# State-space scan kernel: finer preparation of a segment, a second buffer for each product with C, du * B a step ahead, side loads two slots ahead

## Chip, cores and metric

The kernel runs on one core of one Trainium2 chip. The metric is the device time of one execution in microseconds. Every profile line comes from one profiled execution; TensorE is called PE, VectorE DVE, ScalarE ACT, GpSimd POOL, and SP is the engine whose queue issues the DMAs.

## What is computed

The reference is a network of four layers over four images of 64 x 64 positions with 96 channels. Layers 0 and 1 are selective state-space blocks: a projection, a depthwise 3 x 3 convolution with SiLU, four scans over the positions (rows and columns, each forwards and backwards), a layer norm, a gate and an output projection. Layer 1 works on a Fourier transform of the image. Layers 2 and 3 are linear attention and a feed-forward net on the tokens. Nearly all time goes into the scans, which compute for each channel, with 16 states n:

```
delta = softplus(dts + bias)
h[n]  = h[n] * exp(delta * A[n]) + delta * u * B[n]
y     = sum over n of h[n] * C[n]
```

All is float32 but parts of layers 2 and 3.

## The kernel before

**Phases.** The function `scans` runs six phases: two for layer 0 (each holds a pair of images, 64 channels of each on the 128 partitions at a time) and four for layer 1 (one image each). Each phase has four scan directions, each cut into segments: eight of 512 positions in layer 0, and 512, 512, 384, 384 and 320 in layer 1. That makes 144 segments. Ahead of the first phase and behind the last, the function `alone` runs work that no scan goes beside.

**Steps.** A segment has 12 steps: four quarters `q` of four states each, by three chunks `c` of channels. In each step, DVE runs four scans (L537): two write `hx`, the states 4q and 4q + 1, two write `hy`, the other two. POOL multiplies `hx` by C into `hcx` (L672), DVE multiplies `hy` by C into `hcy` (L692), and PE adds both, transposed, to the accumulator in PSUM (`accumulate`, L559). The two halves get du * B in different ways. For `hy`, POOL multiplies `du` by a broadcast B straight into the `hy` tile, which the scan then overwrites (`front_b`, L532). For `hx`, ACT scales a transposed copy of `du` by B into `bx` (`make_bx`, L489) for all three chunks of a quarter, and PE transposes it back into PSUM one step ahead (`transposed`, L509). ACT makes the exponentials (L514). POOL keeps the last state of a segment for the next one (`keep_state`, L550).

**Preparation.** While a segment is scanned, the generator `prepare` makes the next one ready: it loads `u` (L418), projects it (PE, L424), copies the result out and stores it (ACT L427, SP L428), makes `delta` (PE L433, ACT L435), takes its softplus, with one table load before and one behind it (L437, L438), transposes B (L443, L447), multiplies `du` (DVE, L451) and transposes that (PE L457, ACT L460). Each `yield` ends a piece.

**Side work.** Projections, the norm and gate, the Fourier transforms and the token layers of other images run as a second generator beside the scans, through `Env.step`. `E.defer` puts an eviction off to the next piece.

**What sets the order.** The four computing engines take their instructions in the order in which this code records them (`manual_schedule`); DMAs on SP are placed by a scheduler as early as their inputs and buffers allow. A step has three slots. In each one, `slot` runs a piece of side work when the phase's rate (`RATES`, a third of it a slot) has gathered to 1. `prepare_more` runs a piece of preparation, before the second and third slots. A generator that has yielded `LATE` goes on only in the third slot, and one that has yielded `BURST` only in `burst`, between the two scans of `hx`. The pieces of `make_bx` are taken in two handfuls a step (`take`); what is left in the last step of a quarter is drained at once, just ahead of the transposes that read it. A pool's tile has one buffer unless `bufs` says more: so with `hx`, `hy`, `hcx` and `hcy`, while `ax` and `delta` have two and `bx` four.

Of the kernel before, what the change touches and what calls it, by code (L numbers as in the profile page):

```python
# [6 lines left out]
F32 = mybir.dt.float32  # L7
# [15 lines left out]
SM = 512  # L23
LATE, BURST = "late", "burst"

RATES = [0.67, 1.37, 2.4, 1.64, 1.64, 1.64]
EXP_LN = "natural_log_exp_and_others"


# [66 lines left out]
class Block:  # L96
# [57 lines left out]
    def project(self, E, g, xf, out):  # L154
# [9 lines left out]
        with E.pool(f"{cfg.pre}pj{g}") as sp:  # L164
            for c in range(C):
# [4 lines left out]
                for p0, p1 in cfg.parts:  # L170
# [8 lines left out]
                    def visits(blocks, half, done):  # L179

                        nxt = load(*blocks[0], half)
                        for b, (r, n) in enumerate(blocks):
                            x, nxt = nxt, load(*blocks[b + 1], half) if b + 1 < len(blocks) else None
                            pi = E.psum(f"pi{half}_{nm}_{r}")
                            self.in_proj(pi, wi, half, x, n * 64)
                            E.defer(lambda r=r, n=n, pi=pi: done(r, n, pi))
                            yield
# [76 lines left out]
    def gated(self, E, g, io, out_proj):  # L264
# [5 lines left out]
        with E.pool(f"{cfg.pre}nm{g}") as sp:  # L270
# [18 lines left out]

            todo = iter(tiles)  # L290
            nxt = load(*next(todo))
            yield
            for b, (r, nr) in enumerate(cfg.rows):
                n = nr * 64
# [91 lines left out]
def scans(tc, ctx, phases, ident):  # L386
# [21 lines left out]
    def prepare(z):  # L408


        blk, cfg, k, S, nm = z.blk, z.cfg, z.k, z.S, z.nm
        rows = cfg.NI * cfg.M

        def room():
            return ps.tile([P, 512], F32, name=f"pp_{nm}", tag="pp")

        z.u = u = sp.tile([P, C, SM], F32, name=f"us_{nm}", tag="us")
        nc.sync.dma_start(out=u[:, :, :S], in_=z.ph.io["u"][k % 2][:, :, z.a : z.a + S])  # L418
        z.xd = blk.dram_tile("xd", (rows, SM), nm, bufs=4)
        yield  # L420
        yield
        px = room()
        for c in range(C):
            nc.tensor.matmul(px[:rows, :S], blk.xpw[:, c, k, :], u[:, c, :S], start=(c == 0), stop=(c == C - 1))  # L424
        yield
        xs = sp.tile([P, SM], F32, name=f"xs_{nm}", tag="xs", bufs=2)
        nc.scalar.copy(xs[:rows, :S], px[:rows, :S])  # L427
        nc.sync.dma_start(out=z.xd[:, :S], in_=xs[:rows, :S])  # L428
        yield
        z.delta = sp.tile([P, C, SM], F32, name=f"delta_{nm}", tag="delta", bufs=2)  # L430
        for c in range(C):
            pd = room()
            nc.tensor.matmul(pd[:, :S], blk.dtw[:, k, c * P : (c + 1) * P], xs[:rows, :S], start=True, stop=True)  # L433
            yield
            nc.scalar.activation(z.delta[:, c, :S], pd[:, :S], AF.Identity, bias=blk.dtb[:, c, k : k + 1])  # L435
        yield BURST
        nc.scalar.activation(z.delta[:, :, :S], z.delta[:, :, :S], AF.Softplus)  # L437
        nc.scalar.preload_act_table_set(EXP_LN)  # L438
        yield
        pb = room()  # L440
        pbv = pb[:, : NBK * rows].rearrange("p (b m) -> p b m", b=NBK)
        for i, (t, n) in enumerate(z.blocks):
            nc.tensor.transpose(pbv[:n, i, :], xs[:rows, t : t + n], ident[:rows, :rows])  # L443
        z.bt = sp.tile([P, NBK, rows], F32, name=f"bt_{nm}", tag=f"bt{cfg.pre}", bufs=2)
        yield
        for lo, hi, n in z.runs:
            nc.scalar.copy(z.bt[:n, lo:hi, :], pbv[:n, lo:hi, :])  # L447
        yield
        yield
        z.du = sp.tile([P, C, SM], F32, name=f"du_{nm}", tag="du", bufs=2)  # L450
        nc.vector.tensor_tensor(z.du[:, :, :S], z.delta[:, :, :S], u[:, :, :S], ALU.mult)  # L451
        yield
        z.dut = sp.tile([P, NBK, C, P], F32, name=f"dut_{nm}", tag="dut", bufs=2)
        for c in range(C):
            pt = room().rearrange("p (b d) -> p b d", b=NBK)
            for i, (t, n) in enumerate(z.blocks):
                nc.tensor.transpose(pt[:n, i, :], z.du[:, c, t : t + n], ident)  # L457
            yield
            for lo, hi, n in z.runs:
                nc.scalar.copy(z.dut[:n, lo:hi, c], pt[:n, lo:hi, :])  # L460
# [37 lines left out]
    def drain(gen):  # L498
        for _ in gen:
            pass  # L500
# [96 lines left out]
    with tc.manual_schedule(engines=IN_ORDER):  # L597
        drain(prepare(segs[0]))
        drain(make_bx(segs[0], 0))
        fetch(segs[0], 0)  # L600
        st = steps[0]
        st.px, st.ay = [transposed(st, j) for j in range(2)], {}
        front_x(st)
        front_b(st)
        front_y(st, 0)
        closing = None
        bgen, pgen, pwants, at, due = none, none, None, 0, 0.0

        def prepare_more(kind):

            nonlocal pwants
            if pwants not in (None, kind):
                return False
            pwants = next(pgen, LATE)
            return True

        def slot(kind):

            nonlocal due
            due = min(due + st.z.ph.rate / 3, 3.0)  # L620
            if due >= 1.0:
                due -= E.step(kind)

        def burst():

            if pwants is BURST:
                return prepare_more(BURST)
            if E.wants is BURST:
                E.step(BURST)
                return True  # L630
            return False

        for i, st in enumerate(steps):
            z, q, c, S = st.z, st.q, st.c, st.z.S
            nxt = steps[i + 1] if i + 1 < len(steps) else None
            if q == 0 and c == 0:
                after = segs[at + 1] if at + 1 < len(segs) else None
                if at == 0 or z.ph is not segs[at - 1].ph:
                    if closing:
                        close_chunk(closing)  # L640
                        closing = None
                    z.ph.io["y"] = [z.blk.dram_tile(f"y{j}", (2, z.cfg.L, C * P), z.ph.g) for j in range(2)]
                    E.start(z.ph.side(E))
                open_segment(z, segs[at - 1] if at else None)
                if after and after.ph is not z.ph:
                    E.finish()
                pgen, pwants = prepare(after) if after else none, None
                at += 1
            if c == 0:
                if q + 1 < NQ:  # L650
                    bgen = make_bx(z, q + 1)
                    fetch(z, q + 1)
                elif after:
                    drain(pgen)
                    bgen = make_bx(after, 0)
                    fetch(after, 0)
            per = -(-2 * z.cfg.NI * NBK // C)
            hx = sp.tile([P, 2, SM], F32, name=f"hx_{st.nm}", tag="hx")
            scan(st, hx, 0, st.ax[:, 0], st.px[0], 4 * q)
            front_y(st, 1)  # L660
            if nxt:
                nxt.ay = {}
                front_x(nxt)
            long = burst()
            scan(st, hx, 1, st.ax[:, 1], st.px[1], 4 * q + 1)
            slot(None)
            if nxt:
                if c == C - 1:
                    drain(bgen)
                nxt.px = [transposed(nxt, 0)]  # L670
            hcx = sp.tile([P, 2, SM], F32, name=f"hcx_{st.nm}", tag="hcx")
            nc.gpsimd.tensor_tensor(hcx[:, :, :S], hx[:, :, :S], z.c[q][0][:, :, :S], ALU.mult)  # L672
            keep_state(st, hx, 4 * q)
            first = 0 if long else per - per // 2
            take(bgen, first)
            scan(st, st.hy, 0, st.ay[0], st.hy[:, 0], 4 * q + 2)
            if nxt:
                nxt.px.append(transposed(nxt, 1))
            prepare_more(None)
            slot(None)  # L680
            scan(st, st.hy, 1, st.ay[1], st.hy[:, 1], 4 * q + 3)
            keep_state(st, st.hy, 4 * q + 2)
            if nxt:
                front_y(nxt, 0)
            take(bgen, per - first)
            if closing:
                close_chunk(closing)
            accumulate(st, hcx, 4 * q)
            prepare_more(None)
            slot(LATE)  # L690
            hcy = sp.tile([P, 2, SM], F32, name=f"hcy_{st.nm}", tag="hcy")
            nc.vector.tensor_tensor(hcy[:, :, :S], st.hy[:, :, :S], z.c[q][1][:, :, :S], ALU.mult)  # L692
            if nxt:
                front_b(nxt)
            accumulate(st, hcy, 4 * q + 2)
            closing = st if q == NQ - 1 else None
        close_chunk(closing)
        E.finish()
# [548 lines left out]
```

## Time and profile before

| What | Value |
|---|---|
| Median of 3 runs | 13097.33 us |
| Lowest and highest run | 13086.38 and 13113.72 us |
| Span of the profiled execution | 13109.2 us |
| Mean clock granted to TensorE | 0.841 of full speed |
| First scan starts, last step ends (about) | 528 us, 12551 us |
| POOL L532, du * B into hy | 1728 instructions, 3707.7 us |
| POOL L672, hx * C into hcx | 1637 under this name, 3556.9 us |
| DVE L692, hy * C into hcy | 1636 under this name, 1935.3 us |
| ACT L489, bx | 6272 instructions, 2760.0 us |

The page of the profile gives for each engine the time in which it was busy. For each group of instructions it gives their number, their total and mean duration, and the time in which the engine stood idle just ahead of them, together with the instruction whose end released it. A name such as `hcx_l<-hx_l,bc_l` reads output from inputs, with buffer numbers left out. Since a name that the tracer cuts in another place makes a group of its own, some groups are split (`b_l`, `ab_l`, or `cy_l` for a part of `hcy`). A wait of an engine that others don't wait for costs nothing; so a wait is weighed by what it does to the engine that is full.

### The profile page before, as it was taken

The numbers are of one execution on the slowest core, as the hardware profiler recorded it, in microseconds if no ns is written. First come the engines' busy times: TensorE is split into PE (matmuls) and PEld (weight loads), VectorE is DVE, ScalarE is ACT, GpSimd is POOL, SyncE is SP. The second block draws the span as 40 slices with busy tenths as digits, with TensorE's granted clock in tenths as the row PEclk, the third lists the DMA queues.
The fourth block names the chain that finished last, engine by engine and source line by source line (L and its number), as shares of the span: only waits on it lengthen the run. The fifth ranks groups of instructions, "written<-read, shape, count | busy, mean of one in ns | idle before, by whom it ended". The sixth has DMA issues, their size and how long they took to land. (4 is left out here: it accounts for less than half of the span.)

```text
span 13109.2 us, 165038 instructions
## 1 busy us (share of the span) xinstructions
PE 10013.8 (76%) x54680; PEld 7250.2 (55%) x54680; DVE 10549.6 (80%) x10170; ACT 9044.4 (69%) x17333; POOL 9139.5 (70%) x6620
## 2 busy tenths in 40 slices
PE   5677777777777888777888878877788777887766
PEld 1355555555665656556666555555556555555544
DVE  1398999999999888898776588898988989889833
ACT  1478888887777777886566677677676776767723
POOL 0398888888888887887556577676776767766620
PEclk8788888888888998888888889787887778887775
DMA  4444444444554545444444334322343224332231
GB/s 117 109 127 118 121 121 120 118 115 119 134 139 122 122 127 124 133 118 144 132 115 111 117 127 124 103 82 81 122 119 103 80 80 133 113 101 80 77 96 26
DMA packets 1264705, 1464.41 MB, mean 112 GB/s; under 512 B 494243, under 2 KB 1027055, under 8 KB 1255143
## 3 DMA queue, kind: packets, MB, share of 16 engines
q1 hardware_dynamic: 1263847, 1453.85, 39.6%
q8 instruction: 431, 7.06, 0.2%
q14 instruction: 427, 3.50, 0.1%
HBM read 1217.05 MB, written 236.50 MB: 111 GB/s over the span
## 5 line engine op out<-in xcount | busy, mean ns | idle before, releaser
L532 POOL TENSOR_TENSOR hy_l<-du_l,bc_l 128x1024 f32<-128x1024 f32 (+2 forms) x1728 | 3707.7, 2146 | 1710.9 <-DVE hcy_l L692 1261.0
L672 POOL TENSOR_TENSOR hcx_l<-hx_l,bc_l 128x1024 f32<-128x1024 f32 (+2 forms) x1637 | 3556.9, 2173 | 819.4 <-PE acc_l L559 654.6
L489 ACT ACTIVATE bx_l<-dut_l,bt_l 128x192 f32<-128x192 f32 (+2 forms) x6272 | 2760.0, 497 | 0.2
L692 DVE TENSOR_TENSOR hcy_l<-hy_l,bc_l 128x1024 f32<-128x1024 f32 (+2 forms) x1636 | 1935.3, 1183 | 392.4 <-PE acc_l L559 278.3
L559 PE MATMUL acc_l<-ident,hcy_l 128*128 128x128 f32 (+1 forms) x12120 | 1902.1, 306 | 363.0 <-DVE hcy_l L692 359.9
L514 ACT ACTIVATE ax_l<-delta_l,l_alog 128x512 f32<-128x512 f32 (+2 forms) x3456 | 2139.0, 667 | 0.0
L514 ACT ACTIVATE b_l<-delta_l,l_alog 128x512 f32<-128x512 f32 (+2 forms) x1961 | 1230.4, 628 | 1246.7 <-DVE hx_l L537 809.6
L537 DVE TENSOR_TENSOR_SCAN hy_l<-b_l,state_l,hy_l 128x512 f32<-128x512 f32 (+2 forms) x1697 | 1861.4, 1131 | 284.5 <-POOL hy_l L532 136.4
L559 PE MATMUL acc_l<-ident,hcx_l 128*128 128x128 f32 (+1 forms) x12126 | 1973.8, 314 | 86.5 <-POOL hcx_l L672 81.0
L559 PEld LDWEIGHTS acc_l<-ident,hcy_l 128*128 128x128 f32 (+1 forms) x12120 | 1606.3, 159 | 687.1 <-DVE hcy_l L692 488.2
L537 DVE TENSOR_TENSOR_SCAN hx_l<-ax_l,state_l,b_l 128x512 f32<-128x512 f32 (+2 forms) x1697 | 1839.7, 1125 | 164.1 <-PE b_l L509 132.2
L559 PEld LDWEIGHTS acc_l<-ident,hcx_l 128*128 128x128 f32 (+1 forms) x12126 | 1637.3, 161 | 520.1 <-issue 243.6
L509 PE MATMUL b_l<-ident,bx_l 128*128 128x128 f32 x6872 | 1262.3, 307 | 682.8 <-DVE hy_l L537 312.0
L514 ACT ACTIVATE ab_l<-delta_l,l_alog 128x512 f32<-128x512 f32 x1314 | 906.7, 690 | 937.7 <-DVE hx_l L537 637.4
L550 POOL COPY state_l<-hy_l 128x2 f32<-128x2 f32 x1392 | 1242.0, 892 | 373.2 <-DVE hy_l L537 283.4
L509 PEld LDWEIGHTS b_l<-ident,bx_l 128*128 128x128 f32 x6872 | 859.9, 154 | 1147.4 <-DVE hy_l L537 375.3
L509 PE MATMUL ab_l<-ident,bx_l 128*128 128x128 f32 x5260 | 944.6, 310 | 672.7 <-DVE hy_l L537 255.3
L537 DVE TENSOR_TENSOR_SCAN hy_l<-ab_l,state_l,hy_l 128x512 f32<-128x512 f32 x978 | 1206.2, 1270 | 126.2 <-POOL hy_l L532 75.8
L537 DVE TENSOR_TENSOR_SCAN hx_l<-ax_l,state_l,ab_l 128x512 f32<-128x512 f32 x979 | 1197.8, 1264 | 79.7 <-PE ab_l L509 69.3
L509 PEld LDWEIGHTS ab_l<-ident,bx_l 128*128 128x128 f32 x5260 | 656.1, 155 | 977.4 <-DVE hx_l L537 325.9
L225 PE MATMUL pc_l<-pad_l,l_dg 128*128 128x512 f32 (+2 forms) x1944 | 852.4, 582 | 60.0 <-ACT uh_l L214 43.7
L146 PE MATMUL pi_l<-xi_l,l_wi 96*128 96x384 f32 (+6 forms) x912 | 393.8, 717 | 286.7 <-DMA xi_l<-xn 131.0
(190 smaller groups left out, 12475.2 us busy)
## 6 DMA issues: line engine op xcount, KB each, us to landing
bc_l<-l_xd_l SPq DMA_DIRECT2D x1536, 256.0 KB
bc_l<-l_xd_l SPq DMA_DIRECT2D x384, 512.0 KB
bc_l<-l_xd_l SPq DMA_DIRECT2D x384, 384.0 KB
us_l<-l_u SPq DMA_DIRECT2D x96, 768.0 KB
l_y<-y_l SPq DMA_DIRECT2D x288, 256.0 KB
bc_l<-l_xd_l SPq DMA_DIRECT2D x192, 320.0 KB
yt_l<-l_y SPq DMA_DIRECT2D x264, 192.0 KB
yt_l<-l_y SPq DMA_DIRECT2D x128, 384.0 KB
```

The costliest lines, as they stand in the source:

```text
L146: self.nc.tensor.matmul(out[i * cfg.PI : (i + 1) * cfg.PI, :n], wi[:, ki, half, :], xin[:, max(i, ki), :n], start=(ki == 0), stop=(ki == c ...
L225: nc.tensor.matmul(pc[:, : n * 64].rearrange("p (r w) -> p r w", w=64), diag[:, t, :], pad[:, r - p0 + dy : r - p0 + dy + n, dx : dx + 64] ...
L489: nc.scalar.activation(t[:n, b, :, ch], z.dut[:n, b, :, ch], AF.Copy, scale=z.bt[:n, b, m : m + 1])
L509: nc.tensor.transpose(pb[:, t : t + n], st.z.bx[st.q, j][:n, b, st.c], ident[:n, :n])
L514: nc.scalar.activation(out, z.delta[:, st.c, : z.S], AF.Exp, scale=z.blk.A[:, st.c, z.k, n : n + 1])
L532: nc.gpsimd.tensor_tensor(st.hy[:, :, :S], du, st.z.b[st.q][:, :, :S], ALU.mult)
L537: nc.vector.tensor_tensor_scan(h[:, j, : z.S][:, ::step], a[:, : z.S][:, ::step], b[:, : z.S][:, ::step], 0.0 if z.first else z.state[st.c ...
L550: nc.gpsimd.tensor_copy(z.state[st.c][:, n0 : n0 + 2].rearrange("p (j o) -> p j o", o=1), h[:, :, e : e + 1])
L559: nc.tensor.matmul(z.acc[st.c][:n, b, :], hc[:, j, t : t + n], ident, start=(n0 + j == 0 and b == 0), stop=(n0 + j == NST - 1 and b == 0), ...
L672: nc.gpsimd.tensor_tensor(hcx[:, :, :S], hx[:, :, :S], z.c[q][0][:, :, :S], ALU.mult)
L692: nc.vector.tensor_tensor(hcy[:, :, :S], st.hy[:, :, :S], z.c[q][1][:, :, :S], ALU.mult)
```

## The change

It has five parts. The slots of a step: `slot` now runs a piece of preparation itself, so preparation goes on in all three slots of a step and not in two. `prepare`: one more empty piece behind the load of `u`, one projection matmul a piece, evictions two slots behind their matmuls, and the product `du` only in the third slot of a step. `make_bx`: the next quarter's pieces begin in the last step of the quarter before, and what used to be drained there is then already made; the first segment's second quarter is started ahead of the loop. `hcx` and `hcy` get two buffers. The side work's `visits` and `gated` yield two more times behind their first loads, and the rates are a little higher.

```diff
-RATES = [0.67, 1.37, 2.4, 1.64, 1.64, 1.64]
+RATES = [0.71, 1.42, 2.55, 1.66, 1.66, 1.66]
...
                         nxt = load(*blocks[0], half)
+                        yield
+                        yield
...
             nxt = load(*next(todo))
+            yield
+            yield
             yield
...
         z.xd = blk.dram_tile("xd", (rows, SM), nm, bufs=4)
         yield
         yield
+        yield
         px = room()
         for c in range(C):
             nc.tensor.matmul(px[:rows, :S], blk.xpw[:, c, k, :], u[:, c, :S], start=(c == 0), stop=(c == C - 1))
+            yield
         yield
...
             nc.tensor.matmul(pd[:, :S], blk.dtw[:, k, c * P : (c + 1) * P], xs[:rows, :S], start=True, stop=True)
+            yield
             yield
...
         z.bt = sp.tile([P, NBK, rows], F32, name=f"bt_{nm}", tag=f"bt{cfg.pre}", bufs=2)
         yield
+        yield
...
         yield
         yield
+        yield LATE
         z.du = sp.tile([P, C, SM], F32, name=f"du_{nm}", tag="du", bufs=2)
...
-        bgen, pgen, pwants, at, due = none, none, None, 0, 0.0
+        bgen, pgen, pwants, at, due = make_bx(segs[0], 1), none, None, 0, 0.0
...
             nonlocal due
+            prepare_more(kind)
             due = min(due + st.z.ph.rate / 3, 3.0)
...
                 if q + 1 < NQ:
-                    bgen = make_bx(z, q + 1)
                     fetch(z, q + 1)
...
                 if c == C - 1:
                     drain(bgen)
+                    if q + 2 < NQ:
+                        bgen = make_bx(z, q + 2)
+                    elif q + 1 == NQ:
+                        bgen = make_bx(nxt.z, 1)
                 nxt.px = [transposed(nxt, 0)]
-            hcx = sp.tile([P, 2, SM], F32, name=f"hcx_{st.nm}", tag="hcx")
+            hcx = sp.tile([P, 2, SM], F32, name=f"hcx_{st.nm}", tag="hcx", bufs=2)
...
-            prepare_more(None)
             slot(None)
...
-            prepare_more(None)
             slot(LATE)
-            hcy = sp.tile([P, 2, SM], F32, name=f"hcy_{st.nm}", tag="hcy")
+            hcy = sp.tile([P, 2, SM], F32, name=f"hcy_{st.nm}", tag="hcy", bufs=2)
```

## The prediction, made before the result was known

> **What bounds the kernel now.** I read the busy shares first, then busy time by phase, then who VectorE (DVE) waited for, and last two stretches of the order of time.
>
> The page's shares, and the answer for six stretches that run from the first scan of one phase to the first scan of the next (columns: stretch, its length, then PE, PEld, DVE, ACT, POOL busy with counts, granted PE clock, DMA share, GB/s):
>
> ```profile
> PE 10013.8 (76%) x54680; PEld 7250.2 (55%) x54680; DVE 10549.6 (80%) x10170; ACT 9044.4 (69%) x17333; POOL 9139.5 (70%) x6620
> ```
>
> ```profile
> 528.00:3144.00 2616.00, 1935.64 (x10761) 1385.16 (x10760) 2408.77 (x1993) 2114.75 (x4152) 2298.07 (x1505) 0.88 0.44 118
> 3144.00:5901.00 2757.00, 2156.55 (x12596) 1655.88 (x12596) 2445.08 (x2041) 2166.13 (x4256) 2271.65 (x1512) 0.89 0.49 128
> 5901.00:7739.00 1838.00, 1528.21 (x7894) 1110.72 (x7894) 1324.35 (x1310) 1157.82 (x2045) 1152.89 (x937) 0.83 0.43 123
> 7739.00:9345.00 1606.00, 1235.37 (x7048) 904.78 (x7047) 1397.88 (x1487) 1130.81 (x2147) 1127.67 (x866) 0.83 0.34 102
> ```
>
> DVE is the fullest engine in every scan phase but the third, where PE (1528 of 1838 us) passes it. DVE stands idle 207, 312 and 514 us in the first three phases and 208 in the fourth; the last two are like the fourth (209 and 214). Together that is some 1660 us of 13109: the most that better feeding of DVE could ever return. The other 1090 us lie before the first scan (528) and after the last (558), where nothing of the change acts.
>
> DVE in order of time, two undisturbed steps of 512 (columns: start, length, operation, count, idle before and its releaser):
>
> ```profile
> 5385.17 2.46 DVE L537 TENSOR_TENSOR_SCAN hy_l<-b_l,state_l,hy_l 128x512 f32<-128x512 f32 x2
> 5387.74 1.23 DVE L692 TENSOR_TENSOR hcy_l<-hy_l,bc_l 128x1024 f32<-128x1024 f32 x1
> 5388.88 2.45 DVE L537 TENSOR_TENSOR_SCAN hx_l<-ax_l,state_l,b_l 128x512 f32<-128x512 f32 x2
> 5391.49 2.46 DVE L537 TENSOR_TENSOR_SCAN hy_l<-b_l,state_l,hy_l 128x512 f32<-128x512 f32 x2 [0.17 <-POOL hy_l L532]
> ```
>
> From scan to scan 5391.49 - 5385.17 = 6.32 us: DVE runs back to back but for 0.17. What stretches other steps is in the waits of DVE within the scans (who, for whom: us in total, times, longest):
>
> ```profile
> DVE hy_l L537 <- POOL hy_l L532: 304.7, 1298, 2.3
> DVE hcy_l L692 <- PE acc_l L559: 278.3, 172, 9.0
> DVE hy_l L537 <- ACT b_l L514: 163.5, 136, 12.4
> DVE hx_l L537 <- PE b_l L509: 146.9, 86, 5.9
> DVE xr L884 <- PE pio L879: 104.5, 32, 6.2
> DVE xr L763 <- PE po L755: 97.6, 28, 6.7
> DVE hx_l L537 <- PE ab_l L509: 83.3, 39, 9.0
> DVE hy_l L537 <- ACT ab_l L514: 64.3, 61, 3.8
> ```
>
> The first is the 0.17 of each undisturbed step. The 278.3 is the wait for the single hcy buffer. The 146.9 + 83.3 = 230.2 are scans of hx that wait for the transposes of bx. One such stall on PE, from its order of time:
>
> ```profile
> 5353.86 0.48 PE L509 MATMUL b_l<-ident,bx_l 128*128 128x128 f32 x1 [7.20 <-ACT bx_l L489]
> 5354.55 0.47 PE L509 MATMUL b_l<-ident,bx_l 128*128 128x128 f32 x1 [0.21 <-ACT bx_l L489]
> 5354.96 3.35 PE L146 MATMUL pi_l<-xi_l,l_wi 96*128 96x448 f32 x4
> 5358.11 1.91 PE L559 MATMUL acc_l<-ident,hcx_l 128*128 128x128 f32 x8
> 5359.81 1.91 PE L559 MATMUL acc_l<-ident,hcy_l 128*128 128x128 f32 x8
> 5361.52 0.68 PE L509 MATMUL b_l<-ident,bx_l 128*128 128x128 f32 x3
> ```
>
> The last bx pieces of a quarter stood on ACT behind a Silu with two table loads; PE idled 7.20 us, and side work, accumulation and the next transposes queued behind. In the same stretch DVE idled 2.61 us ahead of hx and 3.08 ahead of hcy. The last line also matters: the transposes that the next hx scan needs follow the accumulation of hcy at once on PE.
>
> **What the Trainium skill says.** "Perfetto Trace Analysis", section Optimization Strategy, says that the same gap repeating on the engine that should be full can mean too few buffers. The trace agrees as to the place (172 waits at L692, and 654.6 us in 280 waits of POOL at L672 for PE to free hcx), but not as to the size for DVE: 278.3 of some 1660 us. "SBUF — State Buffer", section SBUF: two separate sides, says that a DVE operation with two SBUF inputs and a GpSimd one exclude each other for a whole instruction. The trace agrees: hcy of 128x1024 takes 1225 ns as a median and 1282 as a mean over 1152, and reaches 3372 at most; it is long where a late hcx is still on POOL. "ScalarE: Activation LUTs", section What ACT_TABLE_LOAD costs, gives some 1283 ns for a load; the trace shows the same 1283 at L437.
>
> **The change part by part.** No instruction is added or removed; the slots only meet different pieces.
>
> (a) bx a step earlier. A quarter has 16 pieces in the first block (6 a step, 4 drained in the last step, just ahead of the transposes that need them) and 8, 6 or 6 in the second (3 a step, 2 drained at 512). Started a step earlier, nothing is left to drain except in the quarter that opens a segment. ACT does the same 2760 us of bx, so the gain is only that PE doesn't wait. PE and its weight loads idled 749 us before bx transposes until ACT bx, both counted (286 on PE's own row); most was slack. On DVE I take half of the 230.2 us of hx waits, 115, the rest being PE's own lag, and 15 of the hcy waits that follow such a stall. Sum 130; bounds 30 and 250.
>
> (b) Two buffers for hcx and hcy. An hcy wait ends when the accumulation of a step before is done; the transposes for the next hx follow on PE within 0.9 us of that, plus a first-slot piece where there is one. hcy itself takes 1.23. So a wait taken away returns mostly as a wait of the next hx scan: where no piece lies between, it saves some 0.3 to 0.7 us. 172 waits by 0.3 us are 52 of the 278.3. The early hcx (654.6 us of POOL) is worth what hcy loses to the collision: (1282 - 1225) ns by 1152, 66 us, some 83 with the shorter shapes by the same ratio; I take 48. Sum 100; bounds 40 and 300.
>
> (c) Preparation: 25 pieces at three a step instead of 16 at two; it ends in the ninth step instead of the eighth, before it is needed in the tenth. The three projections at L424 (2.74 us together in the trace) go to PE one a slot, and the copies that ACT waited for (228.3 us at L427, 212.1 at L435, mostly since PE hadn't got there) stand two slots later, so ACT is on time with the exponentials that hy waits for (163.5 + 64.3). Most of those waits come from the Softplus of the segment, table load 1.28, activation 1.49, table load 1.28, some 4.05 us in one piece, which stays, only a step later. I take a quarter of 228, 57, say 60; bounds -80 and 120. Below nothing, because a piece now runs in a step's first slot too, ahead of the next transposes. The xs store on SP, the du product on DVE and the broadcasts behind them keep their order and have two steps to spare.
>
> (d) Side loads with two empty slots behind them. PE waited 131 us for xi from xn, mostly before the scans, and some 60 for xi and 23 for yt within. SP has them anyway; only slots move. The rates rise by 1 to 6%, so that the 4 to 26 more slots of a phase's side task fit; counted from the code, each task ends within a segment of where it did, and at most 6 pieces are left for the end of a phase (5 now). Worth 40 us where PE is fullest; bounds 0 and 90.
>
> Sum: 130 + 100 + 60 + 40 = 330 us of the profiled span, 13109 - 330 = 12779. The runs' median, 13097.33, lies 12 below that span: forecast **12770 us**, 2.5% less.
>
> **The rivals.** *The wait only moves.* PE is the bound wherever DVE stands, and its queue order is unchanged, so hx waits replace hcy waits; only the low ends of (a) and (b) and half of (c) come: 30 + 40 + 30 = 100, 13097 - 100, some 13000 us. For it: the third phase, PE at 83%, and the last PE line shown. Against it: the 7.20 us idle on PE. *More comes.* PE's idle time is what makes it late, and each microsecond returned is one that DVE doesn't wait; the upper bounds of (a), (b) and half of (d): 250 + 300 + 45 = 595, some 12500 us. *Slower: first-slot preparation holds up the transposes.* Four of a segment's PE pieces (a projection of 2.74 / 3 = 0.91 us, a delta product at L433 of 1.02 that also waits for ACT's copy, and two sets of transposes like L457's 0.66) now precede the transposes for the next hx. From the end of hx to the next hx there are 2.46 + 1.23, 3.7 us at 512 and some 2.6 at 320. If PE regularly arrives there with more behind it than that minus 0.6 for the transposes, each piece is lost: 0.91 + 1.02 + 0.66 + 0.66 = 3.25 us by 143 segments, 465, against half the gain: 13097 + 465 - 165, some 13400 us. Against it: the undisturbed steps, where PE waits for DVE before most transposes (312.0 + 255.3 us for hy, 249.8 + 220.4 for hx). *It doesn't act*: excluded for (a), since the drained pieces vanish from the order on ACT; for (b) a second buffer is real.
>
> **How the numbers follow.** Forecast, 12650 to 12890: 0.52. The wait only moves, 12890 to 13070: 0.24. More comes, below 12650: 0.17. Slower: 0.07. The measurement can tell some 0.2% (26 us) from no change; 0.04 of the second case lies within that. So faster 0.89, same 0.04, slower 0.07. The range reaches from the upper bounds (12500) past the second case's value (13020); left out are the slower case (0.07), the upper end of the second (0.06) and the tail of the third (0.06).
>
> **What would show it.** (a) right: ACT bx all but gone from PE's waits, hx waits at L537 for PE at half. (b) right: L672 and L692 no longer wait for PE, the mean of hcy near 1240 ns; but hx's wait for PE must not grow by as much. (c) right: ACT's waits at the xs and delta copies under 150 us, hy's wait for ACT somewhat less. (d) right: xi and yt gone from PE's waits in the scans. The first, second and fourth to sixth phase lose some 80, 100 and 30 us each, the third 60. Wrong if the hx wait for PE rises above 400 us: then the queue order of PE decides, not buffers.

## The result, and the profile after

The changed kernel takes 12910.6 us as a median (four runs, 12896.3 to 12925.6) against 13095.8 for the kernel before: a ratio of 0.9857, with a 95% interval of 0.984 to 0.9874. That is 1.43% or some 187 us less. The forecast was 2.5% less, 12770 us; the measured time lies inside the range (12500 to 13020), but in the band that the prediction gave to its first rival, the wait only moves (12890 to 13070), and not in the forecast's own (12650 to 12890). The profiled span fell by 200 us, from 13109.2 to 12908.9.

The busy shares of the page after, and the busy time in the same stretches, from one phase's first scan to the next one's (columns as before):

```profile
PE 9942.2 (77%) x54680; PEld 7205.1 (56%) x54680; DVE 10425.9 (81%) x10170; ACT 9022.7 (70%) x17333; POOL 9126.6 (71%) x6620
```

```profile
530.00:3100.00 2570.00, 1902.44 (x10760) 1377.55 (x10760) 2384.29 (x1992) 2108.62 (x4153) 2281.47 (x1505) 0.89 0.45 120
3100.00:5746.00 2646.00, 2118.34 (x12599) 1634.75 (x12600) 2418.91 (x2042) 2160.44 (x4259) 2269.96 (x1513) 0.90 0.51 134
5746.00:7563.00 1817.00, 1515.24 (x7890) 1093.60 (x7889) 1303.43 (x1309) 1153.07 (x2044) 1183.04 (x937) 0.84 0.43 125
7563.00:9163.00 1600.00, 1247.88 (x7049) 913.08 (x7047) 1378.91 (x1487) 1129.16 (x2148) 1120.50 (x866) 0.83 0.34 102
```

The phases of layer 0 gave 46 and 111 us, the third 21, the fourth 6 (and the last two 1 and 13). The more surprising figure is in the first fence: DVE has the same 10170 instructions, but it is busy for 123.7 us less (10549.6 before). So of the 200 us, nearly two thirds are not waits that went, but operations that got shorter. Only the other 76 are less idle time. In the phases this idle time of DVE falls only in layer 0, by 22 and 85 us; in the third phase it stands still, and in the last three it rises by 13, 16 and 3.

Even these 76 us are not waits of the kind that was forecast. The list of DVE's waits leaves out gaps of up to 0.15 us; what it lists adds up to 2402.0 us before and 2401.0 after. It is the short gaps that went, from 151.5 to 75.9 us in total, and most of them stood ahead of hcy (behind the last bar: DVE's idle time ahead of the group, and how much of it is listed as a wait for which releaser):

```profile
L692 DVE TENSOR_TENSOR hcy_l<-hy_l,bc_l 128x1024 f32<-128x1024 f32 (+2 forms) x1636 | 1935.3, 1183 | 392.4 <-PE acc_l L559 278.3
```

```profile
L704 DVE TENSOR_TENSOR hcy_l<-hy_l,bc_l 128x1024 f32<-128x1024 f32 (+2 forms) x1636 | 1857.5, 1135 | 43.7
```

The idle time falls by 348.7 us here, and only 278.3 of it was listed as a wait for PE. The median gap ahead of an hcy goes from 104 to 34 ns, and the semaphore instructions that DVE's queue runs at this line from 1841 to 530.

What DVE waits for within the scans after the change (who, for whom: us in total, times, longest):

```profile
DVE hx_l L546 <- PE b_l L518: 353.3, 146, 11.5
DVE hy_l L546 <- POOL hy_l L541: 294.4, 1205, 2.5
DVE hy_l L546 <- ACT b_l L523: 141.7, 138, 4.5
DVE hx_l L546 <- PE ab_l L518: 124.4, 62, 7.2
DVE xr L896 <- PE pio L891: 104.1, 35, 6.1
```

The wait of hcy for PE is gone from the list. The waits of hx for the transposes of bx, 230.2 us under these two names before, are 477.7 now. With a third, split name (`_l`) they are 231.6 before and 502.2 after, and the tables below count so. The waits have moved to the next scan, almost to their full length. Counted whatever the releaser, hcy's waits fall by 293 us and those of hx rise by 343, from 287 to 630. What got shorter, by the durations of two DVE lines (minimum/median/maximum in ns), first before, then after:

```profile
L692 DVE TENSOR_TENSOR hcy_l<-hy_l,bc_l x1636: 811/1225/3372, 532.8 to 12555.7; 128x1024 f32<-128x1024 f32 x128, 128x768 f32<-128x768 f32 x35, 128x640 f32<-128x640 f32 x19
```

```profile
L704 DVE TENSOR_TENSOR hcy_l<-hy_l,bc_l x1636: 814/1224/1733, 534.5 to 12359.8; 128x1024 f32<-128x1024 f32 x128, 128x768 f32<-128x768 f32 x35, 128x640 f32<-128x640 f32 x19
```

```profile
L451 DVE TENSOR_TENSOR du_l<-delta_l,us_l x144: 1128/1732/3887, 514.7 to 12427.2; 128x1536 f32<-128x1536 f32 x96, 128x1152 f32<-128x1152 f32 x32, 128x960 f32<-128x960 f32 x16
```

```profile
L460 DVE TENSOR_TENSOR du_l<-delta_l,us_l x144: 1129/1732/1920, 516.4 to 12244.7; 128x1536 f32<-128x1536 f32 x96, 128x1152 f32<-128x1152 f32 x32, 128x960 f32<-128x960 f32 x16
```

The medians stand still and the maxima fall from 3372 to 1733 and from 3887 to 1920. Summed over all instructions, hcy goes from 2022.1 to 1942.4 us and du from 254.4 to 227.8: together 106 us. These two have two inputs in SBUF. They used to run into the hcx of POOL that had waited for its buffer. The longest hcy before, first POOL, then DVE:

```profile
2612.73 3.13 POOL L672 TENSOR_TENSOR hcx_l<-hx_l,bc_l 128x1024 f32<-128x1024 f32 x1 [4.54 <-PE acc_l L559]
```

```profile
2611.91 1.73 DVE L451 TENSOR_TENSOR du_l<-delta_l,us_l 128x1536 f32<-128x1536 f32 x1
2613.57 3.37 DVE L692 TENSOR_TENSOR hcy_l<-hy_l,bc_l 128x1024 f32<-128x1024 f32 x1
```

POOL had waited 4.54 us for the buffer. Then hcx, begun while du ran, took 3.13 us instead of some 2.36, and hcy, begun while hcx ran, ended 1.1 us after it. That is the rule in the trace before: 130 of the 1728 hcy took over 1.15 times the median of their shape; each of them began while POOL ran an operation, 115 times hcx, and ended within 0.15 us of that operation's end plus its own median. After the change there are 12, two of them beside hcx. Of the 144 du 21 were long, all beside an hcx, and none is after.

Where the hx waits come from now can be seen in a stretch of the third phase, first PE, then DVE, in order of time:

```profile
7209.30 2.74 PE L227 MATMUL pc_l<-pad_l,l_dg 128*128 128x512 f32 x6
7211.88 0.82 PE L568 MATMUL acc_l<-ident,hcy_l 128*128 128x128 f32 x6
7212.63 0.84 PE L429 MATMUL pp_l<-us_l,l_xpw 128*44 128x384 f32 x2
7213.40 2.84 PE L227 MATMUL pc_l<-pad_l,l_dg 128*128 128x512 f32 x6
7216.08 0.82 PE L518 MATMUL b_l<-ident,bx_l 128*128 128x128 f32 x6
```

```profile
7209.42 0.99 DVE L704 TENSOR_TENSOR hcy_l<-hy_l,bc_l 128x768 f32<-128x768 f32 x1
7216.70 1.92 DVE L546 TENSOR_TENSOR_SCAN hx_l<-ax_l,state_l,b_l 128x384 f32<-128x384 f32 x2 [6.30 <-PE b_l L518]
```

Between the accumulation of hcy and the transposes that hx needs stand the two pieces of the first slot: a projection of the preparation (0.84 us) and a part of a convolution (2.84). A part like it, from the slot before, holds up the accumulation first. DVE waits 6.30 us.

### The profile page after: what moved, and what is told of

Its sections match the earlier page's. It is cut to its first block, busy times and chain, and to the rows that moved or that the text cites. A ratio compares the mean times of both kernels' runs of the same rounds, so it can differ in the third digit from the quotient of the medians.

```text
span 12908.9 us, 162342 instructions
## 1 busy us (share of the span) xinstructions
PE 9942.2 (77%) x54680; PEld 7205.1 (56%) x54680; DVE 10425.9 (81%) x10170; ACT 9022.7 (70%) x17333; POOL 9126.6 (71%) x6620
## 4 chain that ended last, share of the span: by engine, by line
PE 24%; DVE 23%; ACT 21%; POOL 20%; issue 7%; DMA 5%; SPq 0%; POOLq 0%; DVEq 0%; ACTq 0%
POOL hy_l L541 13%; DVE hy_l L546 12%; DVE hx_l L546 5%; PE pc_l L227 4%; ACT ax_l L523 4%; PE acc_l L568 4%; ACT bx_l L498 4%; POOL state_l L559 4%; DVE hcy_l L704 4%; POOL hcx_l L686 2%; ACT b_l L523 2%; PE b_l L518 2%; ACT ab_l L523 2%; PE pp_l L439 2%; PE pi_l L146 1%
## 5 line engine op out<-in xcount | busy, mean ns | idle before, releaser
L704 DVE TENSOR_TENSOR hcy_l<-hy_l,bc_l 128x1024 f32<-128x1024 f32 (+2 forms) x1636 | 1857.5, 1135 | 43.7
L559 POOL COPY state_l<-hy_l 128x2 f32<-128x2 f32 x1392 | 1365.4, 981 | 574.8 <-DVE hy_l L546 553.3
L518 PE MATMUL ab_l<-ident,bx_l 128*128 128x128 f32 x5260 | 901.8, 307 | 520.9 <-DVE hy_l L546 266.5
L439 PE MATMUL pp_l<-xs_l,l_dtw 76*128 76x512 f32 (+3 forms) x864 | 525.2, 693 | 194.4 <-ACT delta_l L442 181.9
```

The lines of the kernel that those rows point to most:

```text
L518: nc.tensor.transpose(pb[:, t : t + n], st.z.bx[st.q, j][:n, b, st.c], ident[:n, :n])
L559: nc.gpsimd.tensor_copy(z.state[st.c][:, n0 : n0 + 2].rearrange("p (j o) -> p j o", o=1), h[:, :, e : e + 1])
```

## The experiments

The theory after this reading (A, later D): the buffers are worth most for keeping POOL out of DVE's way; the rest is ruled by what stands in PE's queue ahead of the transposes for hx. The rivals: that the waits went for good (B), that a part does nothing or costs (C), that PE has a fixed amount of work whatever its order (E). All ratios are to the kernel before, on the same chip; the waits come from one profiled execution of each version.

**Each part alone, put into the kernel before.** The edits are the parts of the change's own diff:

```diff
 e1: hcx and hcy: tag="hcx", bufs=2 and tag="hcy", bufs=2
 e2: make_bx(z, q + 2) or make_bx(nxt.z, 1) in a quarter's last step
 e3: prepare's new yields, prepare_more(kind) inside slot
 e4: two yields in visits and gated, RATES
```

> The kernel before with two buffers for hcx and hcy and nothing else. Theory A (a wait that the buffers take away mostly returns as a wait of the next hx scan for its transposes, since these follow the accumulation of hcy in PE's queue; what is kept is that hcy no longer runs into a late hcx): about 100 us less, 12980 to 13020; the hcy waits for PE (278 us before) go to 0, the hx waits for PE (230 before) rise to 380 or more, and busy time of the hcy line falls by some 80 us. Theory B (the buffers are the gain, the waits go for good): 12910 or below, with hx waits for PE under 260 us. Theory C (the buffers give nothing): within 0.2% of before.

> The kernel before with bx begun a step earlier and nothing else. Theory A: PE's waits for ACT bx (286 us on its own row) go to under 40, but the hx waits for PE fall only a little, as PE is then late for other reasons: 40 to 80 us less, 13020 to 13060. Theory B (PE's lag is made by bx): 130 us less or more, 12970 or below. Theory C: no change.

> The kernel before with the finer preparation in three slots and nothing else. Theory A (a little less waiting of ACT for projections and delta products, 440 us before, hardly reaches DVE): 0 to 50 us less, 13050 to 13100. Theory B (it is a main part of the gain): 80 us less or more. Theory C (a piece in the first slot holds up the transposes for hx): slower, 13120 or above, with more hx waits for PE.

> The kernel before with the two empty slots behind the side loads and the new rates, and nothing else. Theory A: PE's waits for xi and yt within the scans (some 80 us) go, and 0 to 40 us of it reach the end: 13060 to 13100. Theory B (a denser side task costs DVE more waits for PE than the loads give): 13110 or above.

| Kernel | Median us | Ratio (interval) | hx waits for PE | hcy waits for PE | hy waits for ACT | PE waits for ACT bx |
|---|---|---|---|---|---|---|
| before | 13097.7 | 1 | 231.6 | 289.6 | 239.7 | 287.0 |
| e1, buffers | 12961.7 | 0.9897 (0.9882 to 0.9911) | 479.4 | 0 | 263.7 | 303.2 |
| e2, bx early | 13021.8 | 0.9945 (0.9932 to 0.9958) | 225.1 | 293.6 | 188.6 | 56.4 |
| e3, preparation | 13059.8 | 0.997 (0.996 to 0.998) | 383.9 | 291.5 | 100.7 | 449.6 |
| e4, side loads | 13073.2 | 0.998 (0.9972 to 0.9989) | 298.2 | 261.5 | 217.3 | 311.3 |

e1: The hcy waits of 289.6 us vanish and the hx waits rise by 247.8. Theory A holds for the waits, yet the gain, 1.03% or 135 us, is larger than it said. Whatever the releaser, the hx waits rise by 318, and DVE's listed waits as a whole grow by 46 us. The gain is DVE's busy time, 117.5 us less (hcy by 80.5, du by 26.3), and the short gaps, 75 less.

e2: 0.55%, 72 us. PE hardly waits for bx any more (287.0 to 56.4, where theory A had said under 40), but the hx waits are as long as before. Of DVE's 91 us of listed waits that go, 51 are the wait of hy for ACT's exponentials. The order in the code offers a reason that was not tested apart: the pieces that were drained at once also stood ahead of exponentials. Theory A, with an effect it had not named.

e3: 0.3%, 39 us, in two signs at once. ACT is on time (hy waits 239.7 to 100.7), but the hx waits rise by 152. The first three phases:

```profile
529.00:3167.00 2638.00, 1915.11 (x10758) 1385.46 (x10759) 2412.01 (x1992) 2114.77 (x4151) 2324.29 (x1505) 0.89 0.44 117
3167.00:5966.00 2799.00, 2182.19 (x12600) 1680.89 (x12598) 2450.08 (x2041) 2166.15 (x4257) 2290.04 (x1512) 0.88 0.48 126
5966.00:7782.00 1816.00, 1522.00 (x7895) 1103.86 (x7893) 1320.54 (x1309) 1155.76 (x2045) 1158.00 (x936) 0.84 0.43 125
```

The first grows from 2616 to 2638 us and the second from 2757 to 2799, while the third shrinks from 1838 to 1816. The new preparation puts the softplus into the last step of the second quarter, and without the early bx that is the step in which pieces are drained: four in layer 0, two or none in layer 1. PE's wait for bx of 449.6 us fits that. This part needs the one of e2.

e4: 0.2%, 26 us, as theory A said. PE's wait for yt goes (22.6 to 0 us), that for xi in the scans only in part (60.2 to 41.2).

The four alone give 135 + 72 + 39 + 26 = 272 us, and together 187: they share what they take away.

One rival these tables leave out: TensorE's granted clock. Over the 21 runs of the kernel before beside e1 to e4 it lies between 0.842 and 0.847, and the runs with the higher clock are mostly the shorter ones, by some 5.6 us for each 0.001 (the slope of a straight line through them). e2 and e11 (0.841 to 0.846) have the clock of the kernel before, so their gains don't come from it. e1 has 0.850 on average and e3 0.851, against 0.844: by that slope, an estimate, some 31 of the 135 us of e1 and all 39 of e3 could go with the clock. The shorter operations and gaps of e1 don't: e11 has the first at 0.844, and e3 has neither at 0.851. Whether the clock makes a run shorter, or the order of the work raises the clock, no run here parts.

**One part left out of the changed kernel, and two turns of PE's order.**

```diff
 e5: the changed kernel with prepare and its two calls as before
 e6: tag="hcx") and tag="hcy")
 e7:
-            slot(None)
             if nxt:
...
                 nxt.px = [transposed(nxt, 0)]
+            slot(None)
 e8:
                 nxt.px = [transposed(nxt, 0)]
+            if owed:
+                accumulate(*owed)
...
-            accumulate(st, hcy, 4 * q + 2)
+            owed = (st, hcy, 4 * q + 2)
```

> The changed kernel with the old preparation (pieces in the second and third slots only). Alone, the buffers gave 136 us, bx 76, preparation 38 and side loads 25, together 275, while the whole change gives 187. Theory A (the parts take away the same idle time of DVE, so they overlap evenly): without preparation some 12920 to 12950, a little slower than the whole change. Theory D (preparation in the first slot costs, once hx waits for PE are what binds, since it is queued ahead of the transposes): 12900 or below, no slower than the whole change, with hx waits for PE under 450 us (502 in the whole change).

> The changed kernel with one buffer for hcx and hcy again. Theory A (the buffers' worth is above all that hcy and du no longer run into a late hcx on POOL): busy time of the hcy and du lines is back near 2022 and 254 us, hcy waits for PE near 280, and the time rises by 80 to 140 us over the whole change, 12990 to 13050. Theory B (with bx and preparation spread, PE isn't late any more and the buffers hardly matter): under 12950.

> The changed kernel with the first transposes of bx for the next step recorded ahead of the first slot's pieces, not behind them. Theory D (what is queued ahead of these transposes on PE decides now): hx waits for PE fall from 502 us to under 350, and the time by 50 us or more, 12860 or below. Rival E (PE has a fixed amount of work, and what it doesn't do ahead of the transposes it does behind them, while it idles until the hx scan ends): within 30 us of the whole change, or slower.

> The changed kernel with the accumulation of hcy put behind the next step's first transposes of bx (its second buffer allows that). Theory D: the accumulation, 8 matmuls, some 1 us, no longer stands ahead of the transposes; hx waits for PE fall to under 400 us and the time by 30 us or more. Rival E: PE loses work to do while the hx scans run, and is later with what follows: no gain or slower, with idle time of PE ahead of the transposes up.

| Kernel | Median us | Ratio (interval) | hx waits for PE | hcy waits for PE | PE's transposes wait for hx |
|---|---|---|---|---|---|
| changed | 12910.6 | 0.9857 (0.984 to 0.9874) | 502.2 | 0 | 426.8 |
| e5, without preparation | 12867.8 | 0.9823 (0.9808 to 0.9838) | 528.4 | 0 | 501.0 |
| e6, without buffers | 12988.4 | 0.9915 (0.99 to 0.993) | 260.9 | 225.4 | 469.0 |
| e7, transposes first | 12818.6 | 0.9793 (0.9777 to 0.9808) | 409.1 | 0 | 727.4 |
| e8, hcy accumulated late | 12964.3 | 0.9899 (0.9883 to 0.9916) | 606.4 | 0 | 1454.1 |

e5: The preparation, which alone gave 39 us, seems to cost some 43 inside the change (30 against the repeat, e9). But the hx waits for PE did not fall, as theory D demanded; what is lower is hy's wait for ACT (210.5 to 191.3) and other idle time of DVE. Whatever the releaser, the hx waits are 610 us here and 630 in the changed kernel.

e6: The buffers give 78 us within the change, 135 alone. That is just under the 80 to 140 that theory A said, and even without the buffers hcy's busy time is down to 1994.8 us and du's to 244.1. It fits that PE frees hcx sooner here: POOL waits 497.2 us for it, against 681.4 before.

e7: One line moved gives 92 us more (79 against the repeat, e9, whose clock is nearer: 0.849, and 0.848 here), as D said, though the hx waits fell less than it asked, to 409.1. DVE's listed waits as a whole are 108 us shorter than in the changed kernel. PE now waits 727.4 us for hx at the transposes, 300 more than in the changed kernel, while its waits for hy there fall from 593.8 to 485.6; the time falls all the same: such idling costs nothing where PE isn't late.

```profile
DVE hx_l L546 <- PE b_l L518: 294.2, 171, 8.6
...
DVE hx_l L546 <- PE ab_l L518: 99.0, 62, 6.1
```

e8: Slower than the changed kernel by 54 us, as rival E said. The accumulation was work that PE did while the hx scans ran. Behind the transposes it leaves PE idle, 1454.1 us for hx (and 58.8 for hy, from 593.8):

```profile
PE ab_l L518 <- DVE hx_l L546: 696.4, 349, 8.7
PE b_l L518 <- DVE hx_l L546: 692.7, 382, 7.9
```

How the loss reaches DVE is not shown in full: its hx waits for PE are more (406 for 216) and rise by 104 us, but its listed waits as a whole are 28 us less than in the changed kernel, and its busy time and short gaps 37 and 16 more. A reading that fits e7 and e8, though no run varies the length alone: an order is good when what stands ahead of the transposes is about as long as the scan that releases them. An accumulation of some 1 us fits into it; a convolution piece of 2.84 on top doesn't.

**The last four: the same kernel again, and three that part what was joined.** e10 is e5 with the line of e7 moved, e11 has only `tag="hcx", bufs=2`, and e12 is the kernel before with only the line moved.

> The changed kernel as it is, on the chip of the next three, so that they stand beside it. Both theories: 12890 to 12930, as measured, 1.4% under the kernel before.

> The changed kernel with the old preparation and with the first transposes of bx ahead of the first slot's pieces. Theory D (finer preparation costs because it stands ahead of these transposes in the first slot): with the order turned, old and new preparation are equal within 25 us, so some 12800 to 12840, like the changed kernel with the order alone turned (12819). Theory F (the finer preparation costs in another way, by what it does to ACT after the softplus or by its place in the second and third slots): the old preparation is again 40 us or more ahead, 12780 or below.

> The kernel before with two buffers for hcx alone, one for hcy. Theory A (of the 136 us of both buffers, most comes from POOL being out of DVE's way, and the hcy waits only move to the next hx scan): 80 to 125 us less, 12975 to 13020, with hcy and du lines' busy time down by 80 and 25 us, and hcy waits for PE still near 280 us. Theory B (the hcy buffer counts as much): under 60 us less, 13040 or above.

> The kernel before with only the order turned: first transposes of bx ahead of the first slot's side piece. Theory D in its strong form (this order costs before as well): hx waits for PE fall from 230 to under 150 us and the time by 30 to 90 us. Rival: the single hcy buffer binds first there, the waits move from hx to hcy (above 278), and nothing is gained, within 0.2% of before.

| Kernel | Median us | Ratio (interval) | hx waits for PE | hcy waits for PE |
|---|---|---|---|---|
| e9, changed again | 12897.9 | 0.9843 (0.9829 to 0.9856) | 503.0 | 0 |
| e10, old preparation, transposes first | 12817.7 | 0.978 (0.9767 to 0.9794) | 450.5 | 0 |
| e11, hcx buffer alone | 13016.6 | 0.9938 (0.9925 to 0.995) | 255.0 | 303.8 |
| e12, before, transposes first | 13110.0 | 1.0002 (0.9994 to 1.001) | 180.9 | 323.3 |

e9 repeats the change, 13 us below its first median. The ratio of e5 is 0.2% below the repeat's and 0.34% below the first; its interval is just apart from the first one's and overlaps the repeat's, so the lead of e5 is likely and not more.

e10 and e7 are equal within 1 us in their medians, and within their intervals in the ratios: with the transposes first, the finer preparation neither costs nor gives, to some 20 us, an estimate from the slope above (e10 has the higher clock, 0.852 for 0.848). That speaks for D, and e5's unchanged hx waits against its simple form. How the preparation's cost reaches DVE is left open. One trace of it is in PE's queue: PE's waits for ACT's delta copies, at the preparation's next delta product, are 182.7 and 193.9 us in the changed kernel and its repeat, 103.2 in e5, and 101.6 and 107.5 in e7 and e10, where the two preparations are equal.

e11: The second hcx buffer gives 0.62%, 81 us, with hcy's and du's busy time down by 83.7 and 26.3 us and the hcy waits not less (303.8 for 289.6). The rest of e1's 135, some 54, is what the second hcy buffer adds. It is no wait saved: from e11 to e1 hcy's waits go (307.0 us, whatever the releaser), those of hx and hy rise by 283, and DVE's listed waits as a whole stay (2446.3 and 2447.8). What falls is the short gaps, from 135.2 to 76.7 us, ahead of hcy alone by 66.

e12: In the kernel before, the same line gives nothing. The hx waits fall by 51 and the hcy waits rise by 34:

```profile
DVE hcy_l L692 <- PE acc_l L559: 308.9, 187, 9.5
...
DVE hx_l L537 <- PE b_l L509: 119.3, 69, 4.3
```

The single hcy buffer binds first there. The order pays only in the company of the other parts, 79 to 92 us in e7. That it is the buffers which it needs fits these waits; no run has the order and the buffers alone. The versions of e7 and e10 are 2.1% and 2.2% faster than the kernel before, and 0.5% to 0.8% faster than the changed one.

What the profiled spans are made of, as differences to the kernel before in us (waits: all that are listed for DVE; short gaps: idle time of DVE in gaps of up to 0.15 us):

| Kernel | Span | DVE busy | Short gaps | Waits |
|---|---|---|---|---|
| e1, buffers | -147 | -118 | -75 | +46 |
| e11, hcx buffer alone | -95 | -123 | -16 | +44 |
| e2, bx early | -89 | +1 | +1 | -91 |
| e3, preparation | -43 | -4 | -1 | -39 |
| e4, side loads | -37 | -18 | +4 | -24 |
| changed | -200 | -124 | -76 | -1 |
| e6, without buffers | -136 | -48 | +2 | -90 |
| e7, transposes first | -295 | -112 | -75 | -108 |

The buffers give shorter operations and shorter gaps and lengthen the waits; the other parts take waits away. In the changed kernel the two cancel, and of the kernels in this table only e7, with the order turned, keeps both gains whole.

## Why the prediction was right or wrong

The direction and the range were right; the size was a bit more than half of the forecast, and it came from another place. The forecast put 282 of its 330 us on waits of DVE that go and 48 on hcy's collision with hcx. Of the waits 1 us net is gone; operations of DVE that got shorter gave 124, and gaps too short to be listed, which no term names, gave 76. That these make up over half of the forecast is in part luck.

- **What bounds it.** DVE with some 1660 us idle: right. The phases gave back 74 of them. The text named DVE's idle time as the most that better feeding could return; it left out that DVE's busy time could shrink, although (b) counts on it.
- **(a) bx early, 130 us.** Measured 72 alone. The sign that was named did come (PE's wait for bx from 287.0 to 41.9 in the changed kernel), but the step that took half of hx's 230.2 us for bx was wrong: without the bx waits PE is late for other reasons, and the hx waits stay (225.1 in e2). Over half of what bx gave in waits, 51 of 91 us, came through ACT.
- **(b) buffers, 100 us.** Measured 135 alone. The collision was put at 48 and gave 81 (e11): right in kind, and the mean of hcy of 128x1024 came to 1229 ns, where 1240 was named. The hcy buffer was put at 52 and added some 54, but that is luck: the prediction had each wait come back 0.3 us shorter at the next hx, while they came back in full, and the gain is in the short gaps ahead of hcy. Its condition that hx's wait for PE must not grow by as much was only just met (270.6 against 289.6 us), and is not met when all releasers count (343 against 293). The collision was sized from the mean of hcy alone; the du product, with 26 us, was not seen, nor was the whole of hcy's excess taken.
- **(c) preparation, 60 us.** Alone 39, which may go with the clock; inside the change 30 to 43 lost, if e5's lead holds. ACT's waits at the xs and delta copies fell from 440.4 to 55.8 us, as named, and hy's wait for ACT somewhat. The lower bound (-80, because a piece stands ahead of the transposes) was the side that came true in company.
- **(d) side loads, 40 us.** 26 alone. Of the two waits named, PE's for yt went from 22.6 to 0.6 us and that for xi in the scans only from 60.2 to 46.4.
- **The sum, 330.** This is the step that failed most. The terms were added as though each took away idle time of its own. Alone they gave 272, together 187. The loss is in the waits: bx, preparation and side loads alone take 91, 39 and 24 us of DVE's waits away, the buffers alone add 46, and all together leave them where they were. That the waits do go in e7, with the order of PE's queue turned, fits that this order holds them there.
- **The rivals.** The first, that the wait only moves, was right about the waits: the prediction's own mark for it, hx waits above 400 us, was passed with 502. It left the collision at the low end of (b) and named no short gaps, and so came out at 13000. The slower rival's mechanism is real (the projection ahead of the transposes in the stretch above, and e7), but in that stretch side work is most of what stands there.
- **By phase.** 80, 100, 60 and three times 30 were forecast; 46, 111, 21, 6, 1 and 13 came.

## What to carry to other kernels

When a wait for a buffer is taken away, look in the releasing engine's queue for who waits next: if the next thing that the full engine needs comes right behind, the wait moves by its whole length, and the gain has to be found elsewhere. Compare the maximum and the mean of an operation with its median as well as its waits: a second buffer here was worth more as distance between two engines that block each other than as a wait less. Split a gain into busy time, listed waits and the rest before you explain it. In a queue in order, a piece of filler belongs behind the instructions for which the full engine waits, where that wait is the one that binds (e7, not e12); and savings that end in the same idle time are not added.

## What the runs showed of the hardware

DVE's products with two inputs in SBUF took up to 3372 ns (hcy, median 1225) and 3887 ns (du, median 1732) beside a late product on POOL, and at most 1733 and 1920 once that had its buffer. That agrees with what the Trainium skill, "SBUF — State Buffer", section SBUF: two separate sides, says: a DVE operation with two SBUF inputs and a GpSimd operation that reads SBUF share one pair of ports; the one that starts first holds it for its whole instruction, and the other is blocked. Here it came to 110 us of busy time in 13100 (e11), of which 81 reached the end. POOL's 681.4 us of waiting for PE ahead of hcx stand in no wait of DVE's; they set when hcx ran, and so which of DVE's products it met.

The second buffer of hcy shortened the median gap ahead of an hcy from 104 to 34 ns (104 still in e11, 34 in e1). From e11 to e1 the short gaps ahead of the 1728 hcy fall by 66 us, which no list of waits shows.
